# A fused LoRA projection and routed low-rank FFN: idle-time matmuls at the start, the first weight chunk in quarters, adapters placed through DRAM, and the third x unit loaded sooner

## The chip, the cores and the metric

The kernel runs on one NeuronCore of a Trainium2 chip. A core has five engines that run side by side, each with its own queue of instructions: TensorE (matmul, PE in the profile; its weight loads are shown apart as PEld), VectorE (DVE), ScalarE (ACT), GpSimd (POOL) and SyncE (SP, which here issues transfers). Sixteen DMA engines move data between DRAM and the core's memory SBUF. Matmul results go to PSUM, a small memory that VectorE and ScalarE read. The metric is the device time of one execution in microseconds (us), as the median of several runs; lower is better.

## The reference

The input x has 8 batches of 512 tokens with 2048 features. A linear layer with a per-batch LoRA adapter is followed by a top-1 routed low-rank FFN with 8 experts of rank 16, and the result is added to x:

```python
base = einsum('bti,oi->bto', x, W) + b                 # W: 2048 x 2048
A, Bm = lora_As[mapping], lora_Bs[mapping]             # one adapter (rank 16) a batch
y = base + einsum('btr,bro->bto', einsum('bti,bir->btr', x, A), Bm) * 2.0

logits = einsum('bsd,ed->bse', y, route_w)             # 8 experts
topk_v, topk_idx = top_k(logits, 1)
route_weight = one_hot(topk_idx[..., 0], 8) * topk_v
h = einsum('bsd,erd->bser', y, ffn_A)                  # 8 x 16 = 128 columns
out = x + einsum('bser,eor->bso', route_weight[..., None] * h, ffn_B)
```

Only 136 columns are ever read of y: 128 for the experts and 8 for the logits. All is float32.

## The kernel before

**The fold.** `proj` holds those 136 columns as a matrix of 2048 x 136. Because y is used only through it, the kernel first multiplies W by proj (`cm`, columns R to NA), and the adapters' output side by proj as well (`g4`); then x of 2048 features meets only `cm`, 152 columns with the batch's adapter input side beside them.

W comes in 16 chunks of 128 rows (1 MB each) through four buffers, on SP's queue, with the parts of proj (`pj`) between them (lines 105 to 112). `chunk_w` (L270) regroups a chunk's columns: half on ScalarE, half on VectorE (the copies of L273, into `wv`, two buffers for each half), and then asks for the chunk four further on. `fold_w` (L283) multiplies it: 16 matmuls, 32 instructions in the trace, into the PSUM tiles `pc` (L288). The first chunk's load is in two transfers, each with half of every quarter of a row, so that half of the columns can be regrouped before the rest is there.

**The adapters.** After chunk 2, `load_adapters` (L157) works out row numbers and gathers the adapters with indirect DMAs from GpSimd's queue, and `fill_constants` (L208) writes constants. Between chunks 6 to 9 TensorE transposes one side (`pbT`, L315), VectorE the other (`ad_aT`, L237), and VectorE sums the bias into `bp` (L306, L308). After chunk 11 `project_adapters` (L321) forms `pg`, 128 x 136, whose 128 rows are 8 batches of 16 (L325). The low-rank product of the token loop, `hT`, lies in four quadrants of 32 rows, so each quadrant needs the 16 rows of a batch in its rows 0 to 15, and the bias in row 16. Before the change this is done on TensorE: eight copies mask pg by batch (`gm`, L329), the bias goes through a matmul with `one` (`pb`, L333, copied to `c0q`, L336), and after chunks 12, 13 and 14 `spread_adapters` (L338) multiplies gm by the selection matrix `sel` (`pq`, L342) and adds c0q into g4 (L349).

**The shuffle of x.** x is loaded in 16 units of two tiles (256 tokens, two transfers of 1 MB; L122), in five buffers, of which units 0 and 1 lie in the pool `xpool` from the start and the others in `xpool2`, which takes the place of the pool of W and can be written only after the fold is done. A unit is moved into four quadrants, 16 copies of 32 partitions each (`xq`, L252), shared between ScalarE and GpSimd, and VectorE transposes blocks of it (`turn_x`, L256, the STREAM_TRANSPOSE of L237, into `xT`). Unit 0 is loaded after chunk 8's fold, unit 1 after chunk 10's; unit 0 is shuffled after chunk 12, 4 copies on ScalarE and 12 on GpSimd.

**The token loop.** 32 tiles of 128 tokens, in half steps n (two a tile). In each half step TensorE does half of the 16 `heads` matmuls of tile t (`ph`, L409), and half of `delta` of an earlier tile (`po`, L475). At the end of a tile's heads `turn_low` (VectorE, L421 and L428) builds hT and `add_low` (L433) multiplies it by g4; `route` (VectorE, L446 to L454) picks the expert and weights the row (`wh`); `turn_heads` (TensorE, L464) transposes it, `keep_heads` (ScalarE, L469) copies it to `whT`, `delta` multiplies that by `fb`, and `add_delta` (VectorE, L487) adds to x, which is stored from its own buffer (L496). The order on each engine is the order of the program text: a wait holds all that is behind it on its engine.

`shuffle_slot` (L502) gives the copies of half step n: four of unit (n + 6) // 4, of which ScalarE has 2 (3 in the third slot) and GpSimd the others. The slots n = -2 and -1 are all GpSimd's. Unit 2 has the slots n = 2 to 5.

Of the kernel before, what the change touches and what calls it, by code (L numbers as in the profile page):

```python
# [9 lines left out]
F32 = mybir.dt.float32  # L10
# [8 lines left out]
def kernel(  # L19
# [54 lines left out]
    qpool = ctx.enter_context(tc.tile_pool(name="qpool", bufs=2))  # L74
    tpool = ctx.enter_context(tc.tile_pool(name="tpool", bufs=3))
    small = ctx.enter_context(tc.tile_pool(name="small", bufs=2))
    wctx = ctx.enter_context(ExitStack())
    wpool = wctx.enter_context(tc.tile_pool(name="wpool", bufs=1))
    ps_s = ctx.enter_context(tc.tile_pool(name="ps_s", bufs=2, space=bass.MemoryType.PSUM))
# [1 line left out]

    ctx.enter_context(tc.manual_schedule())


    it_i = const.tile([P, B], I32, name="it_i")
    nc.gpsimd.dma_start(out=it_i, in_=itok.to_broadcast([P, B]))
    pj = wpool.tile([P, NO, NP], F32, name="pj")
    proj_v = proj.rearrange("(c p) e -> p c e", p=P)

    def load_pj(c0, c1):  # L90
        nc.sync.dma_start(out=pj[:, c0:c1, :], in_=proj_v[:, c0:c1, :])

    w_tiles = []

    def load_w(oc, parts=1):
        wt = wpool.tile([P, D], F32, tag="w", bufs=4, name=f"w_{oc}")
        n = DQ // parts
        for k in range(parts):
            nc.sync.dma_start(
                out=wt.rearrange("p (i d) -> p i d", i=NQ)[:, :, ts(k, n)],  # L100
                in_=w[ts(oc, P), :].rearrange("p (i d) -> p i d", i=NQ)[:, :, ts(k, n)],
            )
        w_tiles.append(wt)

    load_pj(0, 1)
    load_w(0, parts=2)
    load_pj(1, 3)
    load_w(1)
    load_pj(3, 5)
# [3 lines left out]

    x_tiles = {}

    xpools = {k: xpool for k in range(2)}

    def load_x(u):
        xt = xpools[u % XB].tile([P, TPU, D], F32, tag=f"x{u % XB}", name=f"x_{u}")
# [5 lines left out]

    ident = const.tile([P, P], F32, name="ident")
    make_identity(nc, ident)
    warm = const.tile([P, 1], F32, name="warm")
    nc.scalar.copy(warm, ident[:, :1])

    own_i = const.tile([P, B], I32, name="own_i")
    nc.gpsimd.iota(own_i, pattern=[[-R, B]], base=0, channel_multiplier=1)
# [67 lines left out]
            )  # L200
        nc.gpsimd.dma_start(out=bias_o, in_=bias)

    sel = const.tile([P, NQ, Q], F32, name="sel")
    one = const.tile([P, NQ, Q], F32, name="one")
    own4 = const.tile([P, NQ], F32, name="own4")
    hls = []

    def fill_constants():  # L208

        s16 = const.tile([P, R], F32, name="s16")  # L210
        nc.vector.tensor_reduce(s16, ident.rearrange("p (b r) -> p r b", r=R), AX.X, ALU.add)
        nc.vector.memset(sel, 0.0)
        nc.vector.tensor_copy(sel[:, :, :R], s16.unsqueeze(1).to_broadcast([P, NQ, R]))
# [54 lines left out]
    wv_tiles = {}  # L268

    def chunk_w(oc):  # L270
        for h, copy in enumerate((nc.scalar.copy, nc.vector.tensor_copy)):
            wv = wpool.tile([P, HJ, P], F32, tag=f"wv{h}", bufs=2, name=f"wv{h}_{oc}")
            copy(  # L273
                wv.rearrange("p j (i a) -> p j i a", a=Q),
                w_tiles[oc].rearrange("p (i j a) -> p j i a", i=NQ, a=Q)[:, ts(h, HJ)],
            )
            wv_tiles[oc, h] = wv
        if oc + 4 < NO:
            if oc in (0, 1):
                load_pj(8 + 4 * oc, 12 + 4 * oc)  # L280
            load_w(oc + 4)
# [33 lines left out]
            nc.tensor.transpose(pt[:, k, :], ad_b[:, ts(4 * g + k, P)], ident)  # L315
        nc.scalar.copy(ad_bT[:, ts(g, 4), :], pt)

    gm = wpool.tile([P, B, NP], F32, name="gm")
    c0q = wpool.tile([P, NP], F32, name="c0q")

    def project_adapters():  # L321

        pg = ps_s.tile([P, NP], F32, tag="s", name="pg")
        for j in range(NO):
            nc.tensor.matmul(  # L325
                pg, ad_bT[:, j, :], pj[:, j, :], start=(j == 0), stop=(j == NO - 1)
            )
        for b in range(B):
            nc.vector.tensor_scalar(  # L329
                gm[:, b, :], pg, mask[:, b : b + 1], COND_SCALING, ALU.mult, ALU.mult  # L330
            )
        pb = ps_s.tile([P, NP], F32, tag="s", name="pb")
        nc.tensor.matmul(  # L333
            pb, one.rearrange("p i s -> p (i s)"), bp, start=True, stop=True
        )
        nc.scalar.copy(c0q, pb)  # L336

    def spread_adapters(b0):  # L338

        n = min(GRP, B - b0)  # L340
        pq = ps_s.tile([P, GRP, NP], F32, tag="s", name=f"pq_{b0}")
        nc.tensor.matmul(  # L342
            pq[:, :n, :],
            sel.rearrange("p i s -> p (i s)"),
            gm[:, b0 : b0 + n, :],
            start=True,
            stop=True,
        )
        nc.vector.tensor_tensor(  # L349
            g4[:, b0 : b0 + n, :],  # L350
            pq[:, :n, :],
            c0q.unsqueeze(1).to_broadcast([P, n, NP]),
            ALU.add,
        )

    chunk_w(0)
    for oc in range(NO):
        if oc + 1 < NO:
            chunk_w(oc + 1)
        fold_w(oc)  # L360
        if oc == 2:
            load_adapters()
            fill_constants()
        if oc == 6:
            nc.sync.dma_start(out=fb, in_=ffn_b)
        if oc in (8, 10):
            load_x((oc - 8) // 2)
        if 6 <= oc < 10:
            turn_adapters(oc - 6)
        if oc in (7, 8):  # L370
            turn(ad_aT, ad_ar, oc - 7)
        if oc in (9, 10):
            fold_bias(range(8 * (oc - 9), 8 * (oc - 8)))
        if oc == 11:
            project_adapters()
        if oc in (12, 13, 14):
            spread_adapters(GRP * (oc - 12))
        if oc == 12:
            shuffle(0, moves[:4], nc.scalar.copy)
            shuffle(0, moves[4:], nc.gpsimd.tensor_copy)  # L380
        if oc == 13:
            for b in range(2):
                nc.scalar.copy(cm[:, :, ds(b * NA, R)], ad_aT[:, :, ts(b, R)])
        if oc == 14:
            for h in range(2):
                turn_x(0, h)
# [1 line left out]
    ps_h = ctx.enter_context(tc.tile_pool(name="ps_h", bufs=2, space=bass.MemoryType.PSUM))  # L388
    ps_o = ctx.enter_context(tc.tile_pool(name="ps_o", bufs=2, space=bass.MemoryType.PSUM))
    xpool2 = ctx.enter_context(tc.tile_pool(name="xpool2", bufs=1))  # L390
    xpools.update({k: xpool2 for k in range(2, XB)})


    ph_tiles = {}
# [97 lines left out]

    def store(t, cols):
        u, k = divmod(t, TPU)
        b, r = divmod(t, TPB)
        nc.sync.dma_start(out=out[b, ts(r, P), cols], in_=x_tiles[u][:, k, cols])  # L496
# [107 lines left out]
```

## Time and profile before

| what | value |
|---|---|
| median of 3 runs | 342.64 us (342.02 to 343.64) |
| the profiled execution | 341.82 us |
| its span, from first to last instruction | 340.0 us |
| granted TensorE clock | 0.999 |
| moved by DMA | 88.48 MB, 260 GB/s over the span |
| chain by engine | PE 92%, DMA 4%, ACT 1%, DVE 1% |
| largest on the chain | heads (L409) 36%, delta (L475) 32%, fold of W (L288) 18% |

The span in forty slices of 8.5 us shows the three stages: the fold up to about 77 us with the DMA engines full until about 65, then the token loop with TensorE full and the others in part.

```profile
PE   0999999999899999999999999999999999999992
PEld 0999999999577777777777777777777777777750
...
PEclk9999999999999999999999999999999999999999
DMA  6999999708933284949494856758494939323226
```

Each digit is a busy share in tenths, 9 for 90% or more; PEclk is the granted clock. The profile names an engine, the source line of the program before, the operation and the tiles (out<-in), then counts and times; in brackets stands the idle time ahead of an instruction and what ended it. What a trace calls a matmul is one of two passes of a float32 matmul.

### The profile page before, as it was taken

How to read it: one execution, taken by the hardware profiler on the slowest of the kernel's cores; microseconds unless marked ns; L12 is line 12 of the kernel's file. 1: busy time of each engine (PE TensorE's matmuls, PEld its weight loads, DVE VectorE, ACT ScalarE, POOL GpSimd, SP SyncE). 2: the span in 40 equal slices, each digit the busy share in tenths (PEclk: the TensorE clock that was granted, in tenths of full speed). 3: DMA queues.
4: the chain of work that ended last, by engine and by line, in shares of the span. 5: the costliest groups of instructions: out<-in, count | busy, mean ns of one | idle time of the engine just before them, and what ended most of it. 6: DMA issues, size and time to landing. Idle time of an engine off the chain costs nothing.

```text
span 340.0 us, 5063 instructions
## 1 busy us (share of the span) xinstructions
PE 322.6 (95%) x1944; PEld 258.0 (76%) x1944; DVE 233.4 (69%) x431; ACT 171.5 (50%) x195; POOL 135.9 (40%) x143
## 2 busy tenths in 40 slices
PE   0999999999899999999999999999999999999992
PEld 0999999999577777777777777777777777777750
DVE  0251562555788888777778888888887787888663
ACT  2222431816856575665766565657566575720000
POOL 2041000999862715380826353453708081600000
PEclk9999999999999999999999999999999999999999
DMA  6999999708933284949494856758494939323226
GB/s 184 403 404 415 414 418 420 319 0 315 421 131 125 123 320 192 374 183 372 160 378 148 348 206 289 255 242 327 169 378 177 373 154 393 132 123 126 123 123 247
DMA packets 15703, 88.48 MB, mean 260 GB/s; under 512 B 1584, under 2 KB 4672, under 8 KB 5440
## 3 DMA queue, kind: packets, MB, share of 16 engines
q1 hardware_dynamic: 15152, 86.05, 64.6%
q0 software_dynamic: 528, 2.11, 1.8%
q8 instruction: 15, 0.25, 0.3%
q14 instruction: 8, 0.07, 0.0%
HBM read 54.60 MB, written 33.55 MB: 259 GB/s over the span
## 4 chain that ended last, share of the span: by engine, by line
PE 92%; DMA 4%; ACT 1%; DVE 1%; issue 0%; DVEq 0%; SPq 0%; ACTq 0%
PE ph L409 36%; PE po L475 32%; PE pc L288 18%; DMA x<-in_x_dram 2%; PE ph L433 2%; DMA w<-in_w_dram 2%; PE pg L325 1%; PE pw L464 1%; ACT xq L252 1%; DVE x L487 1%; PE pq L342 1%; PE pbT L315 1%; ACT wv L273 0%; DVEq L600 0%; ACT cm L298 0%
## 5 line engine op out<-in xcount | busy, mean ns | idle before, releaser
L252 POOL COPY xq<-x 32x1024 f32<-32x1024 f32 x121 | 126.3, 1044 | 139.3 <-DMA x<-in_x_dram 97.2
L252 ACT COPY xq<-x 32x1024 f32<-32x1024 f32 x135 | 140.8, 1043 | 20.1 <-DMA x<-in_x_dram 16.2
L409 PE MATMUL ph<-cm,xT 128*128 128x152 f32 x1024 | 142.7, 293 | 0.5 <-DVE cm L298 0.5
L409 PEld LDWEIGHTS ph<-cm,xT 128*128 128x128 f32 x1024 | 135.2, 190 | 9.3 <-issue 8.6
L475 PE MATMUL po<-fb,whT 128*128 128x512 f32 x256 | 120.3, 593 | 2.0 <-ACT whT L469 1.2
L487 DVE TENSOR_TENSOR x<-x,po 128x1024 f32<-128x1024 f32 (+1 forms) x66 | 77.4, 1176 | 6.9 <-PE po L475 6.9
L237 DVE STREAM_TRANSPOSE xT<-xq 128x1024 f32<-128x1024 f32 x64 | 78.7, 1234 | 0.0
L288 PE MATMUL pc<-pj,wv 128*128 128x136 f32 x512 | 62.4, 283 | 8.4 <-ACT wv L273 8.4
L475 PEld LDWEIGHTS po<-fb,whT 128*128 128x128 f32 x256 | 44.7, 190 | 33.6 <-issue 31.1
L288 PEld LDWEIGHTS pc<-pj,wv 128*128 128x128 f32 x512 | 61.6, 194 | 9.1 <-ACT wv L273 8.4
L469 ACT COPY whT<-pw 128x128 f32<-128x128 f32 x32 | 8.5, 265 | 87.5 <-PE pw L464 87.5
L446 DVE TENSOR_REDUCE top<-ph 128x1 f32<-128x8 f32 x32 | 5.3, 166 | 40.6 <-PE ph L433 40.6
L273 DVE COPY wv<-w 128x1024 f32<-128x1024 f32 x16 | 12.6, 786 | 27.8 <-DMA w<-in_w_dram 25.0
L273 ACT COPY wv<-w 128x1024 f32<-128x1024 f32 x16 | 16.7, 1047 | 26.0 <-DMA w<-in_w_dram 23.2
L433 PEld LDWEIGHTS ph<-g,hT 128*128 128x128 f32 x64 | 12.1, 190 | 14.8 <-issue 13.5
L452 DVE TENSOR_SCALAR rw<-rank,win,top 128x8 f32<-128x8 f32 x32 | 15.3, 478 | 1.2
L433 PE MATMUL ph<-g,hT 128*128 128x136 f32 x64 | 12.6, 279 | 0.0
L464 PEld LDWEIGHTS pw<-ident,wh 128*128 128x128 f32 x32 | 4.5, 141 | 8.2 <-issue 6.0
L428 DVE STREAM_TRANSPOSE hT<-hls 128x128 f32<-128x128 f32 x32 | 10.0, 311 | 1.1
L454 DVE TENSOR_TENSOR wh<-ph,rw 128x128 f32<-128x128 f32 x32 | 9.3, 291 | 1.1
L464 PE MATMUL pw<-ident,wh 128*128 128x128 f32 x32 | 8.8, 274 | 0.3 <-DVE wh L454 0.3
L421 DVE TENSOR_TENSOR hls<-ph,own 128x64 f32<-128x64 f32 x32 | 6.0, 187 | 3.3 <-issue 2.3
(63 smaller groups left out, 63.0 us busy)
## 6 DMA issues: line engine op xcount, KB each, us to landing
x<-in_x_dram SPq DMA_DIRECT2D x32, 1024.0 KB, 8.9
out_dram<-x SPq DMA_DIRECT2D x31, 1024.0 KB, 4.9
w<-in_w_dram SPq DMA_DIRECT2D x15, 1024.0 KB, 11.9
w<-in_w_dram SPq DMA_DIRECT2D x2, 512.0 KB, 6.4
fb<-in_ffn_b_dram SPq DMA_DIRECT2D x1, 1024.0 KB, 12.1
out_dram<-x SPq DMA_DIRECT2D x4, 256.0 KB, 3.2
pj<-in_proj_dram SPq DMA_DIRECT2D x2, 272.0 KB, 11.0
pj<-in_proj_dram SPq DMA_DIRECT2D x2, 136.0 KB, 7.5
```

Source lines behind the costliest of these rows:

```text
L237: nc.vector.transpose(dst[:, ts(h, HJ), :].rearrange("p j (g t) -> p g j t", t=Q), src.rearrange("p g (j a) -> p g j a", a=Q)[:, :, ts(h, ...
L252: copy(xq_tiles[u][ts(i, Q), :, g, :], x_tiles[u][ts(g, Q), :, ts(i, DQ)])
L273: copy(wv.rearrange("p j (i a) -> p j i a", a=Q), w_tiles[oc].rearrange("p (i j a) -> p j i a", i=NQ, a=Q)[:, ts(h, HJ)],)
L288: nc.tensor.matmul(pc[:, k, :], wv_tiles[oc, h][:, j, :], pj[:, oc, :], start=(oc == 0 and k == 0), stop=(oc == NO - 1), skip_group_check= ...
L409: nc.tensor.matmul(ph_tiles[t], xT_tiles[t][:, j, :], cm[:, j, ds(s * R, NA)], start=(j == 0), stop=(j == NJ - 1),)
L428: nc.vector.transpose(hT, h.rearrange("p g s -> p (g s)"))
L433: nc.tensor.matmul(ph_tiles[t][:, ds((1 - b % 2) * R, NP)], hT_tiles.pop(t), g4[:, b, :], start=False, stop=True, skip_group_check=True,)
L452: nc.vector.tensor_scalar(rw, rank, win, top, ALU.is_equal, ALU.mult)
L454: nc.vector.tensor_tensor(wh.rearrange("p (e r) -> p e r", r=R), ph[:, :ER].rearrange("p (e r) -> p e r", r=R), rw.unsqueeze(2).to_broadca ...
L464: nc.tensor.transpose(pw, wh_tiles.pop(t), ident)
L475: nc.tensor.matmul(po[:, k, :], whT_tiles[t], fb[:, ts(h * HN + k, 512)], start=True, stop=True)
L487: nc.vector.tensor_tensor(xs, xs, po[:, ts(m, n)], ALU.add)
```

## The change

Seven things change.

1. A tile `warm` of ones is written by VectorE at the start, and TensorE multiplies it by itself 12 times into an unused PSUM tile, ahead of the first matmul on W. The small first copy of ScalarE now works on this tile, and the matmuls wait for it.
2. W's first chunk is loaded in one transfer of whole rows, the first of SP's queue; the first part of pj is issued from ScalarE.
3. The first chunk is regrouped in four quarters, alternately by VectorE and ScalarE.
4. pb moves ahead of pg, and one VectorE copy spreads it over all of g4. pg is scaled once into `g_sb`, stored to DRAM, and loaded back by four transfers, one for each quadrant, each of which puts 16 rows of every batch side by side in 16 partitions. The masks, the selection matrix, pq and the additions go.
5. Unit 2 of x lies in `xpool` too, and is loaded after chunk 12's fold.
6. The two copies of half step n = 2 that were ScalarE's go to GpSimd.
7. The last tile but one is stored in two halves, each after its own addition.

```diff
+    warm = const.tile([P, P], F32, name="warm")
+    nc.vector.memset(warm, 1.0)
...
-    def load_pj(c0, c1):
-        nc.sync.dma_start(out=pj[:, c0:c1, :], in_=proj_v[:, c0:c1, :])
+    def load_pj(c0, c1, eng=nc.sync):
+        eng.dma_start(out=pj[:, c0:c1, :], in_=proj_v[:, c0:c1, :])
...
-    def load_w(oc, parts=1):
+    def load_w(oc):
         wt = wpool.tile([P, D], F32, tag="w", bufs=4, name=f"w_{oc}")
-        n = DQ // parts
-        for k in range(parts):
-            nc.sync.dma_start(
-                out=wt.rearrange("p (i d) -> p i d", i=NQ)[:, :, ts(k, n)],
-                in_=w[ts(oc, P), :].rearrange("p (i d) -> p i d", i=NQ)[:, :, ts(k, n)],
-            )
+        nc.sync.dma_start(out=wt, in_=w[ts(oc, P), :])
         w_tiles.append(wt)
 
-    load_pj(0, 1)
-    load_w(0, parts=2)
+    load_pj(0, 1, nc.scalar)
+    load_w(0)
...
-    xpools = {k: xpool for k in range(2)}
+    xpools = {k: xpool for k in range(3)}
...
-    warm = const.tile([P, 1], F32, name="warm")
-    nc.scalar.copy(warm, ident[:, :1])
+
+    nc.scalar.copy(warm[:, 1:2], warm[:, :1])
+    pm = ps_s.tile([P, P], F32, tag="s", name="pm")
+    for _ in range(12):
+        nc.tensor.matmul(pm, warm, warm, start=True, stop=True)
...
-        for h, copy in enumerate((nc.scalar.copy, nc.vector.tensor_copy)):
-            wv = wpool.tile([P, HJ, P], F32, tag=f"wv{h}", bufs=2, name=f"wv{h}_{oc}")
-            copy(
-                wv.rearrange("p j (i a) -> p j i a", a=Q),
-                w_tiles[oc].rearrange("p (i j a) -> p j i a", i=NQ, a=Q)[:, ts(h, HJ)],
-            )
-            wv_tiles[oc, h] = wv
+        copies = (nc.scalar.copy, nc.vector.tensor_copy)
+        wv = [
+            wpool.tile([P, HJ, P], F32, tag=f"wv{h}", bufs=2, name=f"wv{h}_{oc}")
+            for h in range(2)
+        ]
+        wr = w_tiles[oc].rearrange("p (i j a) -> p j i a", i=NQ, a=Q)
+        for h in range(2):
+            wv_tiles[oc, h] = wv[h]
+            dst = wv[h].rearrange("p j (i a) -> p j i a", a=Q)
+
+            n = HJ // 2 if oc == 0 else HJ
+            for k in range(HJ // n):
+                copy = copies[1 - k] if oc == 0 else copies[h]
+                copy(dst[:, ts(k, n)], wr[:, ds(h * HJ + k * n, n)])
...
-    gm = wpool.tile([P, B, NP], F32, name="gm")
-    c0q = wpool.tile([P, NP], F32, name="c0q")
+    g_sb = wpool.tile([P, NP], F32, name="g_sb")
+    g_dram = dram.tile([P, NP], F32, name="g_dram")
+
+    def project_bias():
+
+        pb = ps_s.tile([P, NP], F32, tag="s", name="pb")
+        nc.tensor.matmul(
+            pb, one.rearrange("p i s -> p (i s)"), bp, start=True, stop=True
+        )
+        nc.vector.tensor_copy(g4, pb.unsqueeze(1).to_broadcast([P, B, NP]))
...
-        for b in range(B):
-            nc.vector.tensor_scalar(
-                gm[:, b, :], pg, mask[:, b : b + 1], COND_SCALING, ALU.mult, ALU.mult
+        nc.vector.tensor_scalar(g_sb, pg, COND_SCALING, None, ALU.mult)
+        nc.sync.dma_start(out=g_dram, in_=g_sb)
+        for i in range(NQ):
+            nc.sync.dma_start(
+                out=g4[ds(i * Q, R)], in_=g_dram.rearrange("(b r) e -> r b e", r=R)
             )
...
-    def spread_adapters(b0):
...
         if oc == 11:
+            project_bias()
             project_adapters()
-        if oc in (12, 13, 14):
-            spread_adapters(GRP * (oc - 12))
         if oc == 12:
+            load_x(2)
...
-    xpools.update({k: xpool2 for k in range(2, XB)})
+    xpools.update({k: xpool2 for k in range(3, XB)})
...
-        if t < NT - 1 and h == 1:
+        if t == NT - 2:
+            store(t, ts(h, D // 2))
+        elif t < NT - 2 and h == 1:
             store(t, ds(0, D))
...
-    for u in range(2, XB):
+    for u in range(3, XB):
         load_x(u)
...
-        shuffle(u, ms, nc.scalar.copy)
+        shuffle(u, ms, nc.gpsimd.tensor_copy if n == 2 else nc.scalar.copy)
```

In `fill_constants` the five lines that build `sel` go as well.

More of the change, by code (lines that the diff above doesn't have):

```diff
@@ L76 @@
     small = ctx.enter_context(tc.tile_pool(name="small", bufs=2))
+    dram = ctx.enter_context(tc.tile_pool(name="dram", bufs=1, space=bass.MemoryType.DRAM))
     wctx = ctx.enter_context(ExitStack())
@@ L201, in load_adapters @@
         nc.gpsimd.dma_start(out=bias_o, in_=bias)
-    sel = const.tile([P, NQ, Q], F32, name="sel")
     one = const.tile([P, NQ, Q], F32, name="one")
@@ L208, in fill_constants @@
     def fill_constants():
[L210 to L213, printed above, removed]
         nc.vector.memset(one, 0.0)
@@ L327, in project_adapters @@
             )
-        for b in range(B):
-            nc.vector.tensor_scalar(
-                gm[:, b, :], pg, mask[:, b : b + 1], COND_SCALING, ALU.mult, ALU.mult
-            )
[L332 to L336, printed above, removed]
-    def spread_adapters(b0):
[L340 to L354, printed above, removed]
+        nc.vector.tensor_scalar(g_sb, pg, COND_SCALING, None, ALU.mult)
[3 more added lines that the diff above has]
+                out=g4[ds(i * Q, R)], in_=g_dram.rearrange("(b r) e -> r b e", r=R)
+            )
     chunk_w(0)
```

## The prediction

> **What bounds the kernel now.** I read the page's busy row first, then the chain of waits in order of time, then the timeline around its breaks.
>
> ```profile
> PE 322.6 (95%) x1944; PEld 258.0 (76%) x1944; DVE 233.4 (69%) x431; ACT 171.5 (50%) x195; POOL 135.9 (40%) x143
> ```
>
> TensorE is busy for all but 17.4 of 340.0 us. In steady state (100 to 330 us) it works 229.4 of 230.0 us, and the change takes no matmul out there. So gains lie in three places: start, handover from the fold of W to the token loop, and tail. The chain at the start, then at the handover (start us, us, what):
>
> ```profile
> 1.19 6.08 DMA w<-in_w_dram
> ...
> 7.29 1.05 ACT wv L273
> ...
> 8.39 27.67 PE pc L288 x224
> 36.06 0.44 PE pbT L315 x4
> 36.50 3.71 PE pc L288 x32
> ```
>
> ```profile
> 73.24 3.49 PE pc L288 x30
> ...
> 76.75 0.51 ACT cm L298
> ...
> 77.39 8.27 DMA x<-in_x_dram
> ...
> 85.76 1.04 ACT xq L252
> ...
> 87.86 0.17 ACT whT L469
> ...
> 88.07 1.98 PE po L475 x4
> ```
>
> A chunk of W costs TensorE 3.71 us (32 instructions); the first seven take 27.67, not 25.97: 1.70 too much. At the handover unit 2 of x, issued at 77.0, lands at 85.7; two ScalarE copies of it stand ahead of whT, so po starts at 88.07.
>
> Two rows are decisive though they are not on this chain (timeline):
>
> ```profile
> 30.77 1.05 ACT L273 COPY wv<-w 128x1024 f32<-128x1024 f32 x1 [3.80 <-DMA w<-in_w_dram]
> 58.81 25.81 POOL L252 COPY xq<-x 32x1024 f32<-32x1024 f32 x23 [32.00 <-DMA x<-in_x_dram]
> ```
>
> Chunk 6 lands at 30.77 and is regrouped at 31.82; TensorE takes it up at 36.06 - 3.71 = 32.35, a slack of only 0.53. And GpSimd starts 23 back-to-back copies (1.122 us each with gaps) when x unit 0 lands: 12 for unit 0, 11 for unit 1, done at 84.62. The DMA engines are full (share 1.02, about 0.42 MB/us) from 8 to 65 us, so chunk 6 and x unit 0 land by bytes, not by demand. A faster TensorE soon meets both.
>
> **The change, part by part.**
>
> *Start of the W stream.* Chunk 0 becomes one transfer with 8 KB rows, issued at 0.74 instead of two with 1 KB pieces from 1.19; its pj goes out from ScalarE. The windows of the old start and of the restart at 77.0 (8 KB rows into an idle queue); the last two columns are DMA share and GB/s:
>
> ```profile
> 4.00:5.00 1.00, 0.00 (x0) 0.00 (x0) 0.00 (x0) 0.00 (x0) 0.00 (x0) 1.00 0.86 95
> ...
> 77.00:78.00 1.00, 0.57 (x4) 0.60 (x5) 1.00 (x2) 0.97 (x2) 0.96 (x2) 1.00 0.28 33
> 78.00:79.00 1.00, 1.00 (x10) 1.00 (x9) 1.00 (x2) 0.99 (x2) 0.96 (x2) 1.00 0.53 115
> 79.00:80.00 1.00, 1.00 (x10) 1.00 (x9) 0.56 (x1) 0.99 (x2) 0.96 (x2) 1.00 0.99 410
> ```
>
> Old start: 8.39 us at 181 GB/s is 1.52 MB, as if the full 0.42 MB/us had begun at 4.77. Restart: 0.15 MB by 79.0, as if it had begun 1.64 us after its issue; from 0.74 that is 2.4. The GpSimd load of it_i stays, and its packets take 8.6% of the first 10 us, 0.86 us: 3.25. So the stream moves up by **d = 1.5**. Bounds: 0.45 (earlier issue alone, slow phase stays) and 2.4 (it_i costs nothing). I take 1.5, since the restart is the nearest row (same rows, same size). Chunk 0 with its pj is 1.12 MB: 3.25 + 2.67 + 1.2 (the old lag from that byte, 7.45, to the copy at 8.71) = 7.1. A quarter on VectorE is half of its 0.694 us: TensorE starts at 7.55, not 8.39. The other quarters (ScalarE 0.52, VectorE 0.35) come ahead of need at 0.93 us per quarter.
>
> *Warm-up.* Memset on an idle VectorE; ScalarE issues pj (0.4), loads its table (1.28), copies (0.19); TensorE begins at about 2.7: 24 instructions at 0.21 us or less, done at 7.0 to 7.8. Overrunning 7.55 costs up to 0.25. Here rule and row differ. The granted clock reads 1.00 from the first matmul on; by that row warming gives 0. But the spacing is about 0.23 us until 11.8, then 0.116, which makes the 1.70. The Trainium skill (TensorE: Matmul & The Clock Gate, The HAM clock gate) has half clock until some 3.4 us of work, agreeing with the spacing; by it warming gives 1.70. I take 1.70, but it cannot all be kept: from 7.55, chunk 6 is wanted at 7.55 + 6 x 3.71 = 29.8 and ready at 31.82 - 1.5 = 30.3. The stage gains 32.35 - 30.3 = 2.05 instead of 0.84 + 1.70. Chunks 1 to 5 are ready in time; 7 and later have 0.8 or more in the old trace and move with d.
>
> *Adapters through DRAM.* Gone from TensorE: three pq groups, 0.69 + 0.69 + 0.46 = 1.84, all on the chain. Gone elsewhere: 8 gm (2.22), three adds (1.6), one ScalarE copy (0.27), the sel constants (0.73), all beside TensorE. New on VectorE: g4 broadcast from PSUM, 1,088 columns, about 1.2 (x<-x,po: 1,024 in 1.18), in the idle time during pg; g_sb, 0.3, at about 58.4, with copies of chunks 13 to 15 behind it, wanted 3.5 us later. pb moves ahead of pg at the same 0.23. New on SP: a store, then four loads that wait for it, in front of x unit 2 alone. The store queues behind x unit 1 (67.6 - 1.5 = 66.1): landed by about 67.5, loads issued by 69.3 (0.43 each), landed by 72. g4's first reader, L433, comes at 80.9: slack 9. A rule speaks against this: DMA: Bandwidth & Descriptors, Rules for kernel authors, says transfers under 64 KB are mostly overhead and a read of what a DMA wrote must await its completion. Its about 2 us fixed, twice, plus 68 KB is an estimate of 4.3 us; the rows have 1.8 for pj's 68 KB in an empty queue and some 11 in a full one. None fills the 22 us from g_sb to L433, so 0; a round trip beyond 22 us would cost its excess.
>
> *Unit 2 early, two copies to GpSimd.* Issued at about 69.5, landed by 78.5 (8.65 us as before), wanted at 83: the wait for x goes, and whT no longer stands behind it. TensorE's idle time ahead of po goes: from heads to po 9.2 instead of 10.64, 1.44 gained. GpSimd gets 9 copies of unit 2 for 7, 83.1 to 93.2; wanted about 96. Cover 3 us. Units 3 and 4 still wait for the old pools but start with two fewer loads ahead.
>
> *What is late next.* The fold ends at 76.95 - 2.05 - 1.84 = 73.06. x unit 0 lands at 57.3; GpSimd ends its 12 copies at 70.8; VectorE turns them until 73.15 (2.36) and only then copies cm (1.36): heads start at 74.65 (before 77.43). po starts at 83.85 and ends at 85.6. GpSimd ends unit 1 at 57.3 + 25.8 = 83.1; the two turns of unit 1 run to 85.5, then hls and hT (0.5) to 86.0; L433 of tile 1 waits for these. heads of tile 2 start at 86.35 instead of 90.28: **3.93 gained**. From there TensorE is full, as before.
>
> *Tail.* Tile 30 was stored whole after its second half; DMA was idle until 332, then moved 2 MB until 337.5. Its first half now goes 1.1 us earlier, so the quarters of tile 31 no longer queue: last data at about 336.8. **0.65 gained**; bounds 0.2 and 1.1.
>
> Sum: 3.93 + 0.65 = 4.6: span 335.4, execution 341.82 - 4.6 = 337.2. The median, 342.64, lies 0.8 above that execution; the forecast for the median is **338.0 us**. (Heads of tile 2 gain 2.43 + d, so other values of d shift the sum one for one.)
>
> **The rivals.** (A) The forecast: the DMA stream moves up by about 1.5, and GpSimd's chain sets the handover. 0.57.
>
> (B) The slow first phase of DMA is the launch's, not the 1 KB pieces': d = 0.45. For: the restart at 77 also creeps for 2 us. Against: it creeps for 2, not 5. Gain 2.88 + 0.65 = 3.5: **339.1**. 0.22.
>
> (C) The edits add up: 0.84 + 1.70 + 1.84 + 1.44 + 0.65 = 6.5: **336.1**. For: TensorE at 95% says so. Against: the 0.53 slack of chunk 6, and the 23 GpSimd copies. 0.12.
>
> (D) Slower: the DRAM round trip. The four loads touch 16 partitions in 544-byte rows; SP holds x unit 2 behind them. From a landing after 80.9 each us is lost; even is reached at about 85.5, and at 88 both g4 and x unit 2 make it **345**. For: pj took 11 us in a full queue. Against: the queue runs empty at 66. 0.04.
>
> (E) The warm-up does nothing. Then the fold ends 1.2 later, at 74.26, heads start at 75.1, po ends at 86.0, and L433 of tile 1 still waits for hT until 86.0: 338.1 all the same. A time cannot tell this from A; the spacing of the first pc matmuls can. 0.05.
>
> **How the numbers follow.** 338.0 is A's. B and C give 339.1 and 336.1; with the 0.8 between executions the range is 335.9 to 340.2. What a measurement can tell from no change is 0.5%, 1.7 us. A, B, C and E are faster: 0.95 with a little taken off for unnamed mishaps; same 0.03; slower 0.03.
>
> **What would show it.** Right: pc matmuls at 0.116 us from the first; first pc at 7.0 to 8.2; a wait of about 0.5 for chunk 6 near 30; GpSimd starting at about 57.3; VectorE's turn of unit 1 released by GpSimd near 83; no wait of ScalarE for x; last store data near 336.8 minus 3.9. Wrong: GpSimd starting at 58.4 or later (B); no wait at all in the fold and heads at 73 (C); L433 of tile 0 waiting for g4 (D).

## The result, and the profile after

The changed kernel takes 338.03 us (median of 6 runs, 337.86 to 338.20); the kernel before, timed together with it on the same chip, 342.51 us (341.89 to 344.0). The ratio is 0.9861, with a 95% interval of 0.9838 to 0.9884: 1.4% faster. The forecast was 338.0. The profiled execution took 338.08 us with a span of 336.3, against 341.82 and 340.0 before: 3.7 us less. Of all executions below one, of the kernel with the token load late, took 385.55 us at a granted clock of 0.853 and is left out of its ratio.

The busy row and the chain's shares by engine, from the page of the changed kernel:

```profile
PE 324.2 (96%) x1962; PEld 259.9 (77%) x1962; DVE 232.3 (69%) x421; ACT 169.7 (50%) x193; POOL 138.1 (41%) x145
...
PE 77%; DMA 12%; POOL 4%; DVE 2%; issue 1%; ACT 1%; SPq 1%; DVEq 0%; POOLq 0%; ACTq 0%
```

TensorE has 1.6 us more busy time than before (24 warm-up instructions come, three groups of selection matmuls go), and yet its share of the chain that ended last falls from 92% to 77%. Most of the rest has gone to DMA and GpSimd. The same chain in order of time (start us, us, what), from chunk 6 to the third tile:

```profile
32.07 3.97 PE pc L292 x32
...
43.07 14.64 DMA x<-in_x_dram
...
70.82 1.05 POOL xq L249
...
71.90 2.37 DVE xT L234 x2
74.27 1.18 DVE cm L302 x3
...
75.58 6.44 PE ph L400 x48
...
82.95 0.81 DVE rw L443
...
85.50 1.72 PE po L466 x4
...
87.44 2.07 PE ph L400 x16
```

Before, TensorE's fold ran up to 76.75 on this chain. Now the chain leaves TensorE at 40.6, goes through a ScalarE copy of W to the transfer of x unit 0 at 43.07, then through twelve GpSimd copies, two turns and three copies on VectorE, and heads start at 75.58 instead of 77.43. The wait for x unit 2 (8.27 us on the chain before) is gone. heads of tile 2 start at 87.44, before at 90.28: 2.84 us. The other 0.86 us come at the end: from the last add of VectorE to the end of the span it is 3.98 us, before 4.84. The two make the 3.7.

The timeline of the changed kernel for the fold and GpSimd (start us, us, engine, line, instructions; in brackets the idle time ahead and what ended it):

```profile
7.13 3.87 PE L292 MATMUL pc<-pj,wv 128*128 128x136 f32 x32
11.73 15.13 PE L292 MATMUL pc<-pj,wv 128*128 128x136 f32 x128 [0.73 <-ACT wv L281]
27.76 3.97 PE L292 MATMUL pc<-pj,wv 128*128 128x136 f32 x32 [0.91 <-ACT wv L281]
32.07 3.97 PE L292 MATMUL pc<-pj,wv 128*128 128x136 f32 x32 [0.33 <-ACT wv L281]
...
57.89 34.46 POOL L249 COPY xq<-x 32x1024 f32<-32x1024 f32 x31 [32.12 <-DMA x<-in_x_dram]
```

TensorE begins the fold 1.26 us earlier (8.39 before) and at full rate, 3.87 us for a chunk. It then gives 1.97 us back in three waits for chunks 1, 5 and 6, which weren't in the trace before. What is left of the lead can be read from the first instruction behind chunk 6, a transpose of the adapters, in the kernel before and in the changed one:

```profile
35.90 0.60 PE L315 MATMUL pbT<-ident,raw 128*128 128x128 f32 x4
```

```profile
35.88 0.60 PE L319 MATMUL pbT<-ident,raw 128*128 128x128 f32 x4
```

That is 0.02 us. From there the fold ends 1.85 us earlier (75.10, before 76.95), which is the 1.84 of the selection matmuls: in this execution the new start gives TensorE nothing. GpSimd starts 0.92 us earlier (58.81 before).

### The profile page after: what moved, and what is told of

Read it like the earlier page. It is cut to its first block, busy times and chain, and to the rows that moved or that the text cites. A ratio compares the mean times of both kernels' runs of the same rounds, so it can differ in the third digit from the quotient of the medians.

```text
span 336.3 us, 5099 instructions
## 1 busy us (share of the span) xinstructions
PE 324.2 (96%) x1962; PEld 259.9 (77%) x1962; DVE 232.3 (69%) x421; ACT 169.7 (50%) x193; POOL 138.1 (41%) x145
## 4 chain that ended last, share of the span: by engine, by line
PE 77%; DMA 12%; POOL 4%; DVE 2%; issue 1%; ACT 1%; SPq 1%; DVEq 0%; POOLq 0%; ACTq 0%
PE ph L400 39%; PE po L466 32%; DMA w<-in_w_dram 8%; DMA x<-in_x_dram 4%; POOL xq L249 4%; PE pc L292 2%; PE ph L424 2%; PE pw L455 1%; ACT wv L281 1%; DVE xT L234 1%; DVE x L478 1%; DVE cm L302 0%; SPq L101 0%; DVE rw L443 0%; SPq L95 0%
## 5 line engine op out<-in xcount | busy, mean ns | idle before, releaser
L249 POOL COPY xq<-x 32x1024 f32<-32x1024 f32 x123 | 128.5, 1045 | 135.2 <-DMA x<-in_x_dram 102.2
L249 ACT COPY xq<-x 32x1024 f32<-32x1024 f32 x133 | 138.7, 1043 | 20.5 <-DMA x<-in_x_dram 13.6
L292 PE MATMUL pc<-pj,wv 128*128 128x136 f32 x512 | 61.1, 280 | 2.0 <-ACT wv L281 2.0
L292 PEld LDWEIGHTS pc<-pj,wv 128*128 128x128 f32 x512 | 60.0, 190 | 2.6 <-ACT wv L281 2.6
L281 DVE COPY wv<-w 128x1024 f32<-128x1024 f32 (+1 forms) x17 | 12.5, 739 | 33.6 <-DMA w<-in_w_dram 25.6
L281 ACT COPY wv<-w 128x1024 f32<-128x1024 f32 (+1 forms) x17 | 16.8, 996 | 30.6 <-DMA w<-in_w_dram 25.3
L443 DVE TENSOR_SCALAR rw<-rank,win,top 128x8 f32<-128x8 f32 x32 | 16.4, 513 | 1.2
```

The source lines that it names most:

```text
L249: copy(xq_tiles[u][ts(i, Q), :, g, :], x_tiles[u][ts(g, Q), :, ts(i, DQ)])
L281: copy(dst[:, ts(k, n)], wr[:, ds(h * HJ + k * n, n)])
L292: nc.tensor.matmul(pc[:, k, :], wv_tiles[oc, h][:, j, :], pj[:, oc, :], start=(oc == 0 and k == 0), stop=(oc == NO - 1), skip_group_check= ...
L443: nc.vector.tensor_scalar(rw, rank, win, top, ALU.is_equal, ALU.mult)
```

## The experiments

Most expectations set two theories against each other, with the number that each would give in that run. Two views stand behind them: that the handover is set by landings, above all by x unit 0's with GpSimd's copies behind it, so that time saved on TensorE alone is worth little; or that the savings on TensorE come through. Kernels that were not timed together had their own runs of the kernel before beside them (medians 342.5 to 343.4), so it is the ratio that compares throughout. In the table, *x0* is GpSimd's first copy of unit 0, *fold* TensorE's last fold instruction; +17.69 and +0.48 are explained below it; the larger of the two is in bold.

| kernel | time us | ratio to before (95%) | span us | x0 | x0 + 17.69 | fold end + 0.48 | heads start |
|---|---|---|---|---|---|---|---|
| before | 342.51 | 1 | 340.0 | 58.81 | 76.50 | **77.43** | 77.43 |
| after | 338.03 | 0.9861 (0.9838 to 0.9884) | 336.3 | 57.89 | **75.58** | **75.58** | 75.58 |
| no warm-up | 337.93 | 0.9857 (0.9834 to 0.9880) | 336.3 | 57.80 | **75.49** | 74.82 | 75.52 |
| old spread on TensorE | 339.35 | 0.9898 (0.9876 to 0.9920) | 337.6 | 57.60 | 75.29 | **76.61** | 76.61 |
| unit 2 late | 337.96 | 0.9863 (0.9841 to 0.9886) | 336.4 | 57.99 | **75.68** | 74.90 | 75.68 |
| unit 2's copies on ScalarE | 338.19 | 0.9871 (0.9848 to 0.9894) | 336.1 | 57.69 | **75.38** | 74.46 | 75.37 |
| tile 30 stored whole | 338.61 | 0.9868 (0.9848 to 0.9889) | 336.6 | 57.56 | **75.25** | 75.11 | 75.25 |
| before + new front | 341.00 | 0.9937 (0.9916 to 0.9959) | 339.2 | 57.36 | 75.05 | **76.12** | 76.12 |
| token load late | 337.84 | 0.9840 (0.9819 to 0.9862) | 335.9 | 57.22 | **74.91** | **74.92** | 74.92 |
| gathers late | 337.79 | 0.9843 (0.9822 to 0.9865) | 336.0 | 57.61 | 75.30 | **75.42** | 75.42 |
| old front | 339.52 | 0.9899 (0.9882 to 0.9915) | 337.5 | 58.62 | **76.31** | 75.50 | 76.33 |
| gathers and fb late | 337.98 | 0.9854 (0.9838 to 0.9871) | 334.9 | 55.20 | 72.89 | **74.56** | 74.56 |

17.69 us is what lies between GpSimd's first copy and heads in the changed kernel: twelve copies (57.89 to 71.87), two turns and the copies of cm. 0.48 us is TensorE's idle time between the fold's last instruction and heads when only the last copy of cm is between them. In every row heads start at the later of the two, within 0.03 us; in the changed kernel's profiled execution the two fall together, and the chain shown above follows one of them. The handover is a race of two chains, and an edit that shortens one is worth what the other allows.

**No warm-up.**

```diff
-    pm = ps_s.tile([P, P], F32, tag="s", name="pm")
-    for _ in range(12):
-        nc.tensor.matmul(pm, warm, warm, start=True, stop=True)
```

> The changed kernel without its 12 matmuls on the constant. Theory 1 (the fold is held by the arrival of chunks 1, 5 and 6 of W, so a faster TensorE ahead of them only waits longer): first pc at about 6.4, spaced 0.23 until about 9.8, the waits for chunks 1, 5 and 6 shrink or go, chunk 6 starts at 32.1 as with them; time 338.0 to 338.4. Theory 2 (the warm clock is worth its 1.7 on TensorE and something later takes other gains back): chunk 6 starts about 1 later and the time is 339.0 to 339.7.

Time unchanged. The timeline of this kernel (line numbers three lower than in the changed kernel):

```profile
6.50 5.70 PE L289 MATMUL pc<-pj,wv 128*128 128x136 f32 x27 [6.50 <-DVE wv L278]
...
75.52 6.44 PE L397 MATMUL ph<-cm,xT 128*128 128x152 f32 x48 [1.18 <-DVE cm L299]
```

Chunk 0 now begins at 6.50 with 0.211 us per instruction on average (27 in 5.70) instead of 0.121, so the slow phase is real and the warm-up takes it away. It is worth nothing all the same. Its 24 instructions end at 7.1, past chunk 0's readiness at 6.5, and what TensorE gains after that it loses waiting for chunks 1, 5 and 6; here it has no such wait, and its fold ends 0.76 us earlier (74.34 against 75.10), since chunk 6 lands at 30.21 instead of 30.97. And heads follow GpSimd: TensorE idles 1.18 us ahead of them instead of 0.48.

**The old spread on TensorE**, with gm, sel and pq in place of the DRAM round trip:

```diff
-        nc.vector.tensor_scalar(g_sb, pg, COND_SCALING, None, ALU.mult)
-        nc.sync.dma_start(out=g_dram, in_=g_sb)
...
+        for b in range(B):
+            nc.vector.tensor_scalar(
+                gm[:, b, :], pg, mask[:, b : b + 1], COND_SCALING, ALU.mult, ALU.mult
...
+        if oc in (12, 13, 14):
+            spread_adapters(GRP * (oc - 12))
```

> The changed kernel with the adapters spread on TensorE as before (gm, pq, additions), everything else as changed. Theory 1 (these 1.84 are the whole gain of the fold, and the shuffle on GpSimd takes part of it back at the handover): fold ends near 76.9, heads of tile 2 at 88.5 to 88.8 instead of 87.3, time 339.2 to 339.6. Theory 2 (sums add): 339.9.

Against the changed kernel 1.3 us slower in time and in span. GpSimd's chain would have let heads start at 75.29; the three groups on TensorE hold them until 76.61. The edit takes 1.84 us off TensorE and is worth 1.3 of it (76.61 - 75.29). Three kernels timed together with this one, those without the warm-up and with unit 2's edits undone, took 337.93 to 338.19 against its 339.35. In the two profiled executions heads lie only 1.03 us apart, since x unit 0 landed 0.29 earlier here; of the 1.3 between the spans 0.35 lies behind the last add (4.33 us to the end, against 3.98).

**Unit 2 loaded late again**, and, in another kernel, **its two copies on ScalarE again**:

```diff
-    xpools = {k: xpool for k in range(3)}
+    xpools = {k: xpool for k in range(2)}
...
-            load_x(2)
             shuffle(0, moves[:4], nc.scalar.copy)
```

```diff
-            shuffle(u, ms, nc.gpsimd.tensor_copy if n == 2 else nc.scalar.copy)
+            shuffle(u, ms, nc.scalar.copy)
```

> The changed kernel with unit 2 of x loaded late as before, its two copies of half step 2 still on GpSimd. Theory 1 (whT was late only because ScalarE's two copies that waited for x stood ahead of it, so moving them away is enough): x lands near 84.5, whT still at 84.5, time 338.0 to 338.4. Theory 2 (the early load is what pays): po starts 1 or more later, time 339.2 to 339.6.

> The changed kernel with the two copies of half step 2 back on ScalarE, unit 2 still early. Theory 1 (x is there at 77, the copies run in ScalarE's idle time before whT): no wait for x, time 337.8 to 338.3. Theory 2 (they delay whT all the same): 338.8 or more.

Neither changes the time. Either edit alone frees whT: with the early load, ScalarE's copies don't wait; with the copies on GpSimd, a late unit 2 doesn't stand ahead of whT. Both undone at once are found in the kernel before with the new front; its chain (start us, us, what), with line numbers of its own:

```profile
84.78 1.04 ACT xq L252
...
85.84 1.04 ACT xq L252
86.88 0.17 ACT whT L476
...
87.09 1.98 PE po L482 x4
```

From heads to heads of tile 2 it takes 13.19 us by the chain; with the old spread alone, which differs there in these two edits, 11.78. Together they are worth 1.41 us.

**Tile 30 stored whole**, as before the change.

```diff
-        if t == NT - 2:
-            store(t, ts(h, D // 2))
-        elif t < NT - 2 and h == 1:
+        if t < NT - 1 and h == 1:
```

> The changed kernel with tile 30 stored whole as before. Theory 1 (the last 2 MB of stores queue behind the whole store of tile 30): last data 0.6 to 0.9 later against TensorE's end, time 338.6 to 338.9. Rival (the last quarter's own latency sets the end): 338.0 to 338.2.

The end takes 4.62 us from the last add, against 3.98: 0.64 by the trace. This stretch varies between kernels with the same stores: 3.95 to 4.45 us in the eleven traces with tile 30 in halves, 4.62 to 5.01 in the three with it whole. So the edit's worth is clear, its size only to within some tenths. The time is 0.6 above that of the changed kernel, but the two were not timed together, and the ratios (0.9868 and 0.9861) can't tell them apart.

**The kernel before with the new front only**: chunk 0 in one transfer, its pj from ScalarE, regrouped in quarters, and the warm-up.

```diff
-    load_pj(0, 1)
-    load_w(0, parts=2)
+    load_pj(0, 1, nc.scalar)
+    load_w(0)
...
+    for _ in range(12):
+        nc.tensor.matmul(pm, warm, warm, start=True, stop=True)
...
+            n = HJ // 2 if oc == 0 else HJ
+            for k in range(HJ // n):
+                copy = copies[1 - k] if oc == 0 else copies[h]
```

> The kernel before with the front edits alone: matmuls on the constant, whole first chunk, pj from ScalarE, quarters. Theory 1 (adapter gathers in the same DMA queues as chunks 4 to 6 take the earlier start back): chunk 6 taken up within 0.4 of 32.35, fold ends within 0.4 of 76.95, time 342.0 to 342.5. Theory 2 (a worth of its own): 340.4 to 341.

The first theory's number missed: these edits have a worth of their own. heads start 1.31 us earlier (76.12 against 77.43), since chunk 6 lands at 29.68 instead of 30.77 and the fold, which is the later chain here, moves up. The span falls by 0.8, the ratio by 0.6%. Chunk 6 lands at 29.68 to 30.97 in the eight kernels with this front and the gathers after chunk 2, so what the front gives TensorE changes from one to the next: 1.31 us here, 0.02 in the changed kernel.

**The changed kernel with the old front**, the counterpart: the same lines of the diff the other way round, without the warm-up.

> The changed kernel with all front edits undone (no matmuls on the constant, first chunk in two transfers with 1 KB pieces, pj first on SP, halves instead of quarters). Chain theory (heads start 17.7 after x unit 0 lands, as in the eight traces of kernels without pq): x lands near 58.8, heads at 76.5, heads of tile 2 at 88.2, time 338.8 to 339.2; the front edits are worth the 0.9 by which the bytes of x come sooner, not TensorE's 1.7. Rival (TensorE's own loss counts): 339.7 or more.

1.2 us more span, 1.5 more time. The trace has the reason that was expected: x0 is back at 58.62, and heads follow 17.71 later, at 76.33: 0.75 of the 1.2. The other 0.43 lies behind the last add (4.41 us, against 3.98), within the scatter named above. The fold would have allowed 75.50, no later than in the changed kernel. So there the front's worth comes through the earlier bytes of x, not through TensorE. The front alone gives 1.31 at heads, the rest alone 1.10, and both 1.85.

**The token load late.** it_i, whose load goes out first on GpSimd's queue, from SP behind chunk 3 of W:

```diff
-    nc.gpsimd.dma_start(out=it_i, in_=itok.to_broadcast([P, B]))
...
     load_w(3)
+    nc.sync.dma_start(out=it_i, in_=itok.to_broadcast([P, B]))
```

> The changed kernel with the index load it_i (128 rows of 32 bytes) moved from GpSimd's queue to SP's, behind chunk 3 of W. If its small packets make the dip of the DMA rate between 5 and 7 us, the dip goes and chunk 1 lands near 9.4 instead of 10.6. If the dip belongs to the 544-byte rows of pj or to the launch, it stays and chunk 1 lands at 10.4 or later. Time 337.0 to 338.2 in the first case, 337.9 to 338.3 in the second.

The windows show what this load of 4 KB does. First the changed kernel, then this one (us; clock; PE, PEld, DVE, ACT, POOL busy with instructions; granted clock; DMA share; GB/s):

```profile
4.00:5.00 1.00, 1.00 (x7) 1.00 (x6) 0.00 (x0) 0.00 (x0) 0.00 (x0) 1.00 1.04 428
5.00:6.00 1.00, 1.00 (x6) 1.00 (x6) 0.09 (x1) 0.09 (x1) 0.00 (x0) 1.00 1.67 157
6.00:7.00 1.00, 1.00 (x10) 1.00 (x9) 0.67 (x2) 1.00 (x2) 0.00 (x0) 1.00 0.35 89
7.00:8.00 1.00, 1.00 (x11) 1.00 (x10) 0.00 (x0) 0.05 (x1) 0.00 (x0) 1.00 0.97 367
```

```profile
5.00:6.00 1.00, 1.00 (x7) 1.00 (x7) 0.10 (x1) 0.10 (x1) 0.00 (x0) 1.00 1.15 405
6.00:7.00 1.00, 1.00 (x12) 1.00 (x10) 0.67 (x2) 1.00 (x2) 0.00 (x0) 1.00 0.93 393
```

With the load on GpSimd's queue the stream falls from 428 to 157 and 89 GB/s for two microseconds; without it there, it doesn't fall. All nine traces with the new front and this load first have the dip (127 to 191 GB/s, then 35 to 117), and none of the three with the load from SP (404 to 415, then 393 to 412). Place in time and queue changed together, so which of them matters isn't shown. Chunk 1 lands at 9.09 instead of 10.63, and x0 at 57.22 instead of 57.89. The profiled span is 0.4 shorter, the time 0.2: too little to tell from no change. Chunks 4 to 6 land at 21.11, 26.32 and 30.30, and TensorE waits for two of them, so the fold comes in level with GpSimd's chain.

**The gathers late**, after chunk 4 instead of 2, and their turns one chunk later:

```diff
-        if oc == 2:
+        if oc == 4:
             load_adapters()
...
-        if 6 <= oc < 10:
-            turn_adapters(oc - 6)
-        if oc in (7, 8):
-            turn(ad_aT, ad_ar, oc - 7)
+        if 7 <= oc < 11:
+            turn_adapters(oc - 7)
+        if oc in (8, 9):
+            turn(ad_aT, ad_ar, oc - 8)
```

> The changed kernel with the adapter gathers two chunks later (and the transposes that need them one later). Theory 1 (the gathers' 2 MB hold chunks 4 to 6): TensorE's waits for chunks 5 and 6 (0.91 and 0.33) go, fold ends 1.0 to 1.3 earlier, near 74; x unit 0 lands at the same 57.9, GpSimd still ends its shuffle near 84, so heads of tile 2 gain at most 0.4 and the time is 337.5 to 338.0. Theory 2 (W itself is late, whatever else is loaded): waits stay.

Chunks 5 and 6 land at 24.76 and 27.25 (26.66 and 30.97 in the changed kernel) and TensorE waits for neither: the gathers' 2 MB compete with them. The time stays. The warm-up ran until 8.00 in this execution, and the bias sum on VectorE, now later, held TensorE for 1.01 us, so the fold won little; and GpSimd's chain would have held heads until 75.30 anyway.

**The gathers late and fb behind x unit 1.** fb (1 MB, first needed by po) leaves its place ahead of x:

```diff
-        if oc == 6:
-            nc.sync.dma_start(out=fb, in_=ffn_b)
...
             load_x((oc - 8) // 2)
+        if oc == 10:
+            nc.sync.dma_start(out=fb, in_=ffn_b)
```

> The changed kernel with the adapter gathers two chunks later and the 1 MB of fb behind x unit 1. Chain theory: x unit 0 lands near 55.2, GpSimd's chain would let heads start at 72.9, so the fold is the bound again: it ends at 74 to 75, heads start within 0.6 of that end, and the time falls by only 0.5 to 1.3, to 336.8 to 337.6. If heads still start 17.7 after x lands, at 72.9: 335.4. If x is not the cause: 338.0.

x0 comes at 55.20, 2.4 us earlier than with the gathers alone, about what 1 MB takes at 0.42 MB/us (2.5). Now the fold is the later chain and heads start at 74.56. The profiled execution took 336.71 us as the first theory has it; the other three took 337.79, 338.17 and 338.21. Why they are longer is not in the one trace, and it stays open.

**All moves together, first try**: also the token load late, 8 warm-up matmuls instead of 12, and 6 of unit 0's copies on ScalarE instead of 4 (10 on GpSimd).

```diff
-    for _ in range(12):
+    for _ in range(8):
...
-            shuffle(0, moves[:4], nc.scalar.copy)
-            shuffle(0, moves[4:], nc.gpsimd.tensor_copy)
+            shuffle(0, moves[:6], nc.scalar.copy)
+            shuffle(0, moves[6:], nc.gpsimd.tensor_copy)
```

> As v_order, and: the index load behind chunk 3 on SP, 8 instead of 12 matmuls on the constant, and 6 instead of 4 copies of unit 0 on ScalarE. Both bounds come forward: first pc at 6.4 to 6.7, fold ends at 72 to 73 without waits, GpSimd's chain ends by 71; heads at 72.4 to 73.4, time 334.9 to 336.0. If one of them does not move, 336.5 or more.

Missed: 339.16 us, ratio 0.9878 (0.9856 to 0.9901), span 337.5, although x0 was at 54.84. The timeline has two long waits:

```profile
46.01 1.25 DVE L234 STREAM_TRANSPOSE ad_aT<-raw 128x1024 f32<-128x1024 f32 x1 [7.70 <-DMA raw<-in_cond_a_dram,arow_i]
...
57.24 0.47 PE L328 MATMUL pb<-bp,one 128*128 128x136 f32 x2 [2.54 <-DVE bp L312]
```

VectorE waits 7.70 us for a gather, ahead of the turn of ad_aT; the sixteen instructions of the bias sum stand behind it in VectorE's order, and TensorE then waits 2.54 us for the sum. heads start at 76.73. But the wait for the gather is not new: it is 6.64 us in the kernel with the gathers and fb late, where TensorE waited only 0.49 for the sum. What differs is the second half of the sum, first there, then in this kernel:

```profile
51.80 3.12 DVE L312 SCALAR_TENSOR_TENSOR bp<-pj,bias_o,bp 128x136 f32<-128x136 f32 x8
```

```profile
52.44 4.65 DVE L312 SCALAR_TENSOR_TENSOR bp<-pj,bias_o,bp 128x136 f32<-128x136 f32 x8
54.84 33.92 POOL L249 COPY xq<-x 32x1024 f32<-32x1024 f32 x30 [21.27 <-DMA x<-in_x_dram]
```

It begins 0.64 us later, with the gather, and takes 1.53 longer: its last two instructions, which run beside GpSimd's copies, take 1.21 and 1.03 us instead of 0.36. There the sum was done at 54.92, before GpSimd began at 55.20. The two together are the 2.17 us by which heads are later (76.73 against 74.56). So a late gather put the sum where an earlier x made GpSimd run beside it.

**All moves, with the bias sum first.** The gathers after chunk 3, bias_o loaded from SP at the start, and the sum spread over chunks 4 to 7, ahead of the turns of ad_aT:

```diff
+    nc.sync.dma_start(out=bias_o, in_=bias)
...
-        nc.gpsimd.dma_start(out=bias_o, in_=bias)
...
+        if 4 <= oc < 8:
+            fold_bias(range(4 * (oc - 4), 4 * (oc - 3)))
         if oc in (8, 9):
             turn(ad_aT, ad_ar, oc - 8)
-        if oc in (9, 10):
-            fold_bias(range(8 * (oc - 9), 8 * (oc - 8)))
```

> The changed kernel with the GpSimd chain shortened and the bias sum taken off the path. The token load (it_i) goes out on SP behind chunk 3 of W, bias_o on SP behind it, the gathers at chunk 3 (their turns one chunk later), the bias sum (16 instructions on VectorE) at chunks 4 to 7 in place of 9 and 10 and ahead of the turns of ad_aT, fb behind x unit 1, 8 warm-up matmuls in place of 12, and six of the sixteen copies of x unit 0 on ScalarE, ten on GpSimd. If the handover is x unit 0's landing plus GpSimd's copies, as the spans of the other runs say: x unit 0 lands near 55, ten copies of 1.03 to 1.4 us end by 66 to 68, two turns and the cm copies are then ready before TensorE's fold, which ends at 72.5 to 74 without any wait for bp; heads start at 73 to 74.5 (75.58 in the changed kernel), and the time is 335.0 to 336.5. If the time of the executions that are not profiled is set by something that the profiled execution doesn't show (as the run with the gathers and fb moved hints), it stays at 337.5 to 338.5 although the profile shows an earlier handover. If the fold still waits for the bias sum or for the gathers, heads start after 75.5 and the time is 338 or more.

335.92 us (334.55 to 336.19), ratio 0.9781 with an interval of 0.9757 to 0.9805, which lies below that of the changed kernel (0.9838 to 0.9884): faster than both. Its timeline:

```profile
54.81 33.43 POOL L249 COPY xq<-x 32x1024 f32<-32x1024 f32 x30 [25.87 <-DMA x<-in_x_dram]
...
66.67 2.37 DVE L234 STREAM_TRANSPOSE xT<-xq 128x1024 f32<-128x1024 f32 x2 [0.93 <-POOL xq L249]
...
72.62 6.44 PE L400 MATMUL ph<-cm,xT 128*128 128x152 f32 x48 [0.48 <-DVE cm L302]
```

GpSimd's ten copies are done at 66.67, 5.2 us earlier than in the changed kernel, and the turns with them. TensorE runs without a wait from 6.49 to 72.16; only its own work is left in the fold, which is now the later chain. heads start 2.96 us earlier, and the span is 2.8 shorter. What each of the moves gives in this kernel wasn't taken apart, nor whether the warm-up, worth nothing in the changed kernel, is worth something here.

## Why the prediction was right, and where it wasn't

The likeliest case was the right one: GpSimd's copies behind x unit 0 set the handover (alone in five of the variants; in the changed kernel's execution the fold ended level with them), the edits don't add up, and the sum was to be 4.6 us. The profiled execution has 3.7. The forecast for the median, 338.0, met 338.03 by more than its working deserves: the sum promised 0.9 too much, and the 0.8 by which the median of before lay above its profiled execution was added, while in the changed kernel profiled execution and median agree (338.08 and 338.03).

Step by step:

- **d, the W stream moving up: 1.5 forecast, 0.92 measured at x unit 0** (0.82 to 1.45 in the seven others with the new front, it_i first and fb in its place; the mean of the eight is 1.12). The range 0.45 to 2.4 held it, but it lies about half way between the forecast's 1.5 and rival B's 0.45. This is the term of the sum that was mis-sized most, with 0.59 us. The forecast charged it_i's load 0.86 us by its packet time. The run with that load elsewhere has a d of 1.59, outside those 0.82 to 1.45: this points to the load, which now stops a full stream for nearly two microseconds, as the place of a part of what is missing. With such scatter one run doesn't prove the size; in the two kernels with gathers and fb late x0 is at 55.20 with the load first and at 54.84 with it late, only 0.36 apart.
- **GpSimd's chain: 17.35 us from x0 to heads forecast, 17.69 measured.** The forecast took 1.122 us a copy, the mean over 23. The first twelve have 1.165, of which three take 1.40 instead of 1.03, beside VectorE's copies of W (60.52, 64.01 and 67.72, 1.09 to 1.20 us there, 0.69 alone). That is another 0.34 us, and with d it makes the 0.93 by which heads are later than the 74.65 of the forecast.
- **From heads to heads of tile 2: 11.70 forecast, 11.86 by the chain.** The path was not quite as told. rw, 0.29 us alone, took 0.81 beside GpSimd's copies, which cost most of the 0.55 that po came late behind heads. And VectorE's turn of unit 1 was not released by GpSimd near 83: it stood behind wh and began at 84.00. hT was the last to be ready for tile 1, as forecast.
- **Chunk 6: wanted at 29.8, ready at 30.3, a stage gain of 2.05.** It landed at 30.97, later than before the change, and behind it TensorE was 0.02 us ahead of before instead of 2.05. (The forecast read its start before from the modelled end, 36.06 - 3.71; by the spacing of 0.116 back from 35.90 it was 32.19, a slack of 0.37 and not 0.53.) The argument that landings move with d was wrong from chunk 4 on, and chunks 1 and 5, held to be ready in time, were waited for, 0.73 and 0.91 us. With the same front chunk 6 lands at 29.68 to 30.97 where the gathers come after chunk 2, and at 26.64 and 27.25 in the two kernels where they come after chunk 4. The gathers, issued after chunk 2, share the DMA engines with these chunks, and they moved up too (first one issued at 18.73, before at 19.75). So the fold ended at 75.10, not 73.06, level with GpSimd's chain; in the sum it hid.
- **Warm-up: first pc at 7.55 forecast, 7.13 measured; done at 7.0 to 7.8, measured 7.1.** Chunk 0 was ready earlier than forecast (its copies begin at 5.91), so the warm-up overran it. Rival E, that the warm-up does nothing, was tied to a spacing that didn't change. The spacing did change, and the time still doesn't depend on it; that E's time would be the forecast's was right. (E's heads at 75.1 don't follow from its fold: 74.26 + 0.48 is 74.74. Nothing hangs on it.)
- **Adapters through DRAM: 1.84 off TensorE, nothing elsewhere.** Worth 1.3 where the old spread was put back, the rest hidden by GpSimd. Of the round trip nothing shows: the store goes out at 60.63, the loads from 67.97 to 69.72 (69.3 forecast), each landing 2.5 to 2.8 us after its issue, and the first reader of g4 begins at 81.86 with no wait. Rival D is out; the 4.3 us estimated from the rule against small transfers fit into a gap of over 20.
- **Unit 2: 1.44 forecast, 1.41 measured** for both edits together. That each is worth nothing beside the other was not seen.
- **Tail: 0.65 forecast, 0.86 measured**, 0.64 by undoing it alone, with some tenths of scatter in either.

Rival B (d = 0.45, 339.1) and rival C (edits add up, 336.1) lie on either side. C is excluded: a warm-up without worth, a spread worth 1.3 of 1.84. B's mark was a GpSimd start of 58.4 or later; it was 57.89. The range of 335.9 to 340.2 is not quite the sum that it is said to be (0.8 on either side of C and B is 335.3 to 339.9); the result lies inside both.

## What to carry to other kernels

Where two chains of engines meet, put down the end of each, and what an edit gives is the fall of the later one: here heads = the later of x0 + 17.69 and fold end + 0.48 held in twelve kernels to 0.03 us. Bytes that aren't needed soon, in front of the transfer that starts the longer chain, cost their full time on it: 1 MB moved behind it brought x forward by 2.4 us. When a transfer is moved later, look at which in-order engine waits for it and what stands behind that wait, as the bias sum did. When another comes earlier, look at what the engine that it releases will run beside: GpSimd's copies stretched the end of that sum.

## What the runs showed of the hardware

A load of 4 KB from GpSimd's queue took 7.1 us to land and, for two of them, cut a stream of 428 GB/s to 157 and 89; the DMA share read 1.67 and 0.35 in these windows. The same load from SP behind 4 MB of W did no such thing.

The granted clock in these windows reads 1.00 throughout, while TensorE's rate went from 6 instructions a microsecond to 11 between 5 and 8 us. The spacing of the instructions shows the slow phase, the clock's row doesn't. With twelve warm-up matmuls, the fold could begin only at 6.9 to 8.0 us in kernels that begin alike; the Trainium skill (TensorE: Matmul & The Clock Gate, The HAM clock gate) calls the phase variable from run to run, and the scatter between these traces fits that.

How long VectorE's rw (128 x 8 elements) takes depends on whether GpSimd is copying. From the timeline of the changed kernel:

```profile
103.96 0.29 DVE L443 TENSOR_SCALAR rw<-rank,win,top 128x8 f32<-128x8 f32 x1
...
109.67 7.50 POOL L249 COPY xq<-x 32x1024 f32<-32x1024 f32 x7 [7.41 <-ACT xq L249]
...
111.87 1.01 DVE L443 TENSOR_SCALAR rw<-rank,win,top 128x8 f32<-128x8 f32 x1
```

0.29 us with GpSimd idle, 1.01 in the middle of seven of its copies, about the length of one copy (1.03). This is what the Trainium skill (SBUF — State Buffer, SBUF: two separate sides) says of the port pair that VectorE and GpSimd share: held for a whole instruction, and the other blocks; the page says it of some VectorE instructions only, and in these traces the reductions beside the same copies keep their 0.17. The last two instructions of the bias sum in the first try (1.21 and 1.03 us for 0.36) look like the same thing, and the GpSimd copies that take 1.40 beside VectorE's copies of W would be it from the other side. In the forecast each engine's durations were taken as its own.
